# Half B's update gate in a gated recurrent kernel: sigmoid on ScalarE from PSUM, then a transpose on VectorE, in place of one joint transpose and two sigmoids

## The chip, the core and the metric

The kernel runs on one core of one Trainium2 chip. The metric is the device time of one execution in microseconds. Before the change it was 1668.68 us, the median of three runs (1668.61 to 1668.93).

## What is computed

The reference is a recurrent cell over 512 time steps for a batch of 8, with 512 inputs and 512 hidden units, whose states are added to the input:

```python
def step(h, x_t):
    fused = jax.nn.sigmoid(jnp.concatenate([x_t, h], axis=-1) @ w_W + w_b)
    hidden_state, output_state = jnp.split(fused, 2, axis=-1)
    memory_state = x_t @ wx_W + wx_b + hidden_state * (h @ wh_W + wh_b)
    h_new = output_state * h + (1.0 - output_state) * jnp.tanh(memory_state)
    return (h_new, h_new)
_, hs = jax.lax.scan(step, h0, xT)
x = x + jnp.swapaxes(hs, 0, 1)
```

Below, `r` is `hidden_state` before its sigmoid, `z` is `output_state` before its sigmoid, and the h part is `h @ wh_W + wh_b`. Everything is fp32. Each step needs the state of the step before, so 512 steps run one after the other.

## The kernel before the change

**Layouts.** A state is kept transposed, hidden units on the 128 partitions, because TensorE needs it so as its stationary operand. Each matmul has a 128x32 stationary tile, four of them side by side in the four column strips of the array, and its product comes out with batch rows on partitions (32 rows for each strip: 4 steps of a group by 8 batch elements). The gates must therefore be transposed back in blocks of 32x32 before they can be combined with the state; VectorE does that.

**Two halves.** The 512 hidden units are worked on in halves A and B of 256 units, so that one half's elementwise work can run beside matmuls that need the other half only. `hT[0]` is half A's state (hTA in the profile), `hT[1]` is half B's (hTB). The products go to three PSUM tiles for a group of four steps, and the x part of the next groups goes to two more (xp):

- A (256 columns): the h part of half B, the h part of half A from hTA, half A's z and r
- D (128 columns): half B's z (first 64 columns) and half B's r (last 64 columns)
- H (64 columns): the rest of half B's h part

**Order on TensorE.** Line 27 fixes it for every step: `ORDER = "A0 A1 A2 A3 D0 D1 D2 D3 H2 H3"`. The digit is the quarter of the state that is the stationary operand: 0 and 1 are half A, 2 and 3 half B. So A2 is the first matmul of a step that needs half B's new state. Behind H comes one piece of fill (line 397, `products`): x products for later steps, which wait for no state. In six of eight consecutive steps the fill piece is of one size, in the other two it is larger.

**Order on VectorE and ScalarE.** The scheduling is manual (line 187): every engine works off its instructions in the order in which the code issues them. Per step that is lines 485 to 512:

- `turn_r(0)`, `turn_h(0)`, `turn_z(0)`: three transposes of 64 columns out of tile A (tr, md1A, tz); ScalarE takes the sigmoid of each gate half into md0A and hd0A
- `memory(0, 0)`, `memory(0, 1)`: two scans (m<-md0A,md1A) that form r times h part plus x part; ScalarE takes tanh of each
- `turn_part`: a transpose of 64 columns out of A into md1B
- `turn_rz` (lines 455 to 464): one transpose of all 128 columns of D into the tile trz; ScalarE then takes the sigmoid of the r columns (8 of 32 columns, into md0B) and of the z columns (into hd0B), which are 16 elements per partition each
- `update(0, 0)`, `turn_h(1)`, `update(0, 1)`: the first and second scan of half A's new state (hTA<-hd0A,hTA), and between them the transpose of H (md1B<-H)
- `settle(1)` (line 446): a memset of one idle column that waits by semaphore until the transpose of H has written its result. It holds VectorE back until then, because what follows on the same engine reads that result
- `memory(1, 0)`, `memory(1, 1)`: the two scans m<-md0B,md1B, and ScalarE's two tanh behind them
- `update(1, 0)`, `update(1, 1)`: the two scans of half B's new state (hTB<-hd0B,hTB), each of which waits for its tanh

Behind these come pieces of the x work that differ from step to step, two more idle memsets (line 586), and GpSimd's output adds.

**Tiles that the change touches.** A `pair` (line 143) is a tile of 128 partitions by 2 quarters by a number of rows by 2 or 3 slots. hd0B has 8 rows and 3 slots, of which the scan of `update` reads all three, in the memory order row, slot. Its slot 2 holds the sigmoid of -z, that is 1 - sigmoid(z). A transpose into such a slot writes every third 4-byte word; one into half A's md1 (2 slots) writes every second. `IDLE` (line 23) is the width of the tile that the idle memsets write. `DVE_FILL` (line 22) says how many of the pairs are cleared by VectorE at the start.

In the profile one line stands for all uses of a helper: 195 is every matmul, 226 every activation, 403 every scan, 415 the transposes tr and tz, 430 the transposes of the h parts, 447 the settling memsets, 457 trz, 467 the transpose of the h part in A, 265 the transposes of x parts.

Of the kernel before, what the change touches and what calls it, by code (L numbers as in the profile page):

```python
# [7 lines left out]
F32 = mybir.dt.float32  # L8
BF16 = mybir.dt.bfloat16
AF = mybir.ActivationFunctionType  # L10
# [3 lines left out]
P = 128  # L14
NQ = 4
GS = 4
B = 8
HU = 64
# [1 line left out]


DVE_FILL = 23
IDLE = 4
LAST = 4
SYNC = mybir.DependencyInfo(mybir.DependencyClass.Sync, mybir.DependencyReason.DATA)

# [22 lines left out]
def tile_cond_rnn_residual(  # L49
# [39 lines left out]
    nc = tc.nc  # L89
# [7 lines left out]
    work = ctx.enter_context(tc.tile_pool(name="work", bufs=4))  # L97
# [45 lines left out]
    def pair(n, name, rows, slots):  # L143

        return const.tile([P, 2, rows, slots], F32, name=name).rearrange("p c n s -> p n c s")
# [3 lines left out]
    NH = 2 * GS  # L149
    hT = [[pair(n, f"hT{n}{i}", 32, 3) for i in range(NH)] for n in "AB"]  # L150

    md0 = [[pair(n, f"md0{n}{i}", 32, m) for i in range(2)] for n, m in (("A", 2), ("B", 3))]
    md1 = [[pair(n, f"md1{n}{i}", 32, m) for i in range(2)] for n, m in (("A", 2), ("B", 3))]
    hd0 = [[pair(n, f"hd0{n}{i}", B, 3) for i in range(2)] for n in "AB"]
    zeros = const.tile([P, 512], F32, name="zeros")
    nc.vector.memset(zeros, 0.0)
    none = const.tile([P, 128], BF16, name="none")
# [12 lines left out]
    for t_ in hd0[0] + hd0[1]:  # L170
        nc.gpsimd.memset(t_[:, :, :, 1], -1.0)
    idle = const.tile([P, IDLE], F32, name="idle")

# [8 lines left out]
    def state(hf, i, slot=2):  # L182

        s = i % GS
        return hT[hf][i % NH][:, B * s : B * s + B, :, slot]
# [39 lines left out]
    def act(key, out_, in_, func, **kw):  # L225
        inst = nc.scalar.activation(out_, in_, func, **kw).ins  # L226
        if key in written:
            tc.declare_no_dep(inst, written[key], reason="ordered through VectorE")
        written[key] = inst
        return inst  # L230
# [139 lines left out]
    for i in range(T):  # L370
        g, s = divmod(i, GS)
        c, t = divmod(i, TC)
        ps = banks[g % 2]
# [25 lines left out]
        rows = slice(B * s, B * s + B)  # L399

        def scan(c_, out_, d0, d1):

            return nc.vector.tensor_tensor_scan(  # L403
                *[t_[:, :, c_].rearrange("p n c s -> p (n c s)") for t_ in (out_, d0, d1)],
                0.0,
                ALU.mult,
                ALU.add,
            ).ins

        pa = ps["A"][:, HU:] if i else xps[0][:, :HALF]  # L410
        raw = {"h": (pa[:, :HU], ps["H"]), "z": (pa[:, HU : 2 * HU],), "r": (pa[:, 2 * HU :],)}

        def turned(n, hf):
            t_ = work.tile([P, 2, 32], F32, tag=f"t{n}{hf}", name=f"t{n}{hf}_{i}")
            inst = nc.vector.transpose(t_.rearrange("p c n -> p (c n)"), raw[n][hf]).ins  # L415
            return t_[:, :, rows], inst

        h_done = [None, None]

        def turn_r(hf):  # L420
            tr, _ = turned("r", hf)
            act(
                ("r", hf, g % 2, s),
                md0[hf][g % 2][:, rows, :, 1 + hf].rearrange("p n c -> p c n"),
                tr,
                AF.Sigmoid,
            )

        def turn_h(hf):
            inst = nc.vector.transpose(  # L430
                md1[hf][g % 2][:, :, :, hf].rearrange("p n c -> p c n"), raw["h"][hf]
            ).ins
            h_done[hf] = inst
            if hf == 0 and i + 1 - NH in pool_done:
                tc.add_manual_dep(inst, pool_done[i + 1 - NH].name, SYNC)

        def sigma_z(hf, tz):
            act(
                ("zc", hf, i % 2),
                hd0[hf][i % 2][:, :, :, 2].rearrange("p n c -> p c n"),  # L440
                tz,
                AF.Sigmoid,
                scale=-1.0,
            )

        def settle(hf):
            inst = nc.vector.memset(idle[:, IDLE - 2 + hf : IDLE - 1 + hf], 0.0).ins
            tc.add_manual_dep(inst, h_done[hf].name, SYNC)

        def turn_z(hf):  # L450
            tz, _ = turned("z", hf)
            settle(hf)
            sigma_z(hf, tz)

        def turn_rz():
            t_ = work.tile([P, 4, 32], F32, tag="trz", name=f"trz_{i}")
            nc.vector.transpose(t_.rearrange("p c n -> p (c n)"), ps["D"])  # L457
            act(
                ("r", 1, g % 2, s),
                md0[1][g % 2][:, rows, :, 2].rearrange("p n c -> p c n"),  # L460
                t_[:, 2:, rows],
                AF.Sigmoid,
            )
            sigma_z(1, t_[:, :2, rows])

        def turn_part():
            nc.vector.transpose(md1[1][g % 2][:, :, :, 0].rearrange("p n c -> p c n"), ps["A"][:, :HU])  # L467
# [6 lines left out]
        def memory(hf, q):  # L474

            c_ = slice(q, q + 1)
            scan(c_, ms[hf], md0[hf][g % 2][:, rows], md1[hf][g % 2][:, rows])
            act(("n", hf, q, i % NH), state(hf, i, 1)[:, :, c_], ms[hf][:, :, c_, 1 + hf], AF.Tanh)

        def update(hf, q):  # L480
            s1 = (i + 1) % GS
            new = hT[hf][(i + 1) % NH][:, B * s1 : B * s1 + B]
            return scan(slice(q, q + 1), new, hd0[hf][i % 2], hT[hf][i % NH][:, rows])

        turn_r(0)
        turn_h(0)
        turn_z(0)
        memory(0, 0)
        memory(0, 1)
        if i:  # L490
            turn_part()
        turn_rz()
        update(0, 0)
        turn_h(1)
        update(0, 1)
        settle(1)
        if i == 0:

            seed(2)
        memory(1, 0)  # L500
        if i == T - 1:
# [4 lines left out]
                ALU.add,  # L506
            )
        memory(1, 1)
        update(1, 0)
        update(1, 1)  # L510
        for hf in range(2):
# [70 lines left out]
        if i == 4:  # L582
            for to, c_ in ((Q01, slice(256, 448)), (Q23, slice(64, 256))):
                nc.vector.tensor_tensor(step_bias[to], bias[Q23, c_], bias[Q01, c_], ALU.subtract)
        for n in range(IDLE - 2):
            nc.vector.memset(idle[:, n : n + 1], 0.0)
        def add(hf, engine):
            return engine.tensor_tensor(  # L588
# [98 lines left out]
```

## Time and profile before

| what | value |
|---|---|
| time, median of 3 runs | 1668.68 us (1668.61 to 1668.93) |
| the profiled execution: its own time | 1665.8 us |
| the profiled execution: span from first to last instruction | 1664.0 us |
| granted TensorE clock | 1.000 of full speed |
| VectorE busy | 1391.8 us (84%), 10213 instructions |
| ScalarE busy | 1132.3 us (68%), 5884 instructions |
| GpSimd busy | 327.4 us (20%), 1290 instructions |

How to read the rows. A row of the timeline has a start in us, a length in us, the engine, the line, the operation, output<-input, shapes and a count; several instructions of one kind in a row are merged, and their length is that of all of them together. PE is TensorE's matmuls, PEld its weight loads, DVE VectorE, ACT ScalarE. What stands in square brackets is the idle time just before, and what ended it. A row of the groups by line has the total busy time, the mean length of one in ns, and the idle time before. A row of a tile's view has the shortest, median and longest length in ns. Matmuls overlap: four run side by side in the column strips and each is pipelined behind the one before it, so their lengths do not add up. VectorE's and ScalarE's instructions overlap too: the next may start some 0.04 to 0.1 us before the one in front of it has ended.

### The profile page before, as it was taken

How to read it: one execution, taken by the hardware profiler on the slowest of the kernel's cores; microseconds unless marked ns; L12 is line 12 of the kernel's file. 1: busy time of each engine (PE TensorE's matmuls, PEld its weight loads, DVE VectorE, ACT ScalarE, POOL GpSimd, SP SyncE). 2: the span in 40 equal slices, each digit the busy share in tenths (PEclk: the TensorE clock that was granted, in tenths of full speed). 3: DMA queues.
4: the chain of work that ended last, by engine and by line, in shares of the span. 5: the costliest groups of instructions: out<-in, count | busy, mean ns of one | idle time of the engine just before them, and what ended most of it. 6: DMA issues, size and time to landing. Idle time of an engine off the chain costs nothing.

```text
span 1664.0 us, 113147 instructions
## 1 busy us (share of the span) xinstructions
PE 1650.5 (99%) x47566; PEld 1272.1 (76%) x47566; DVE 1391.8 (84%) x10213; ACT 1132.3 (68%) x5884; POOL 327.4 (20%) x1290
## 2 busy tenths in 40 slices
PE   8999999999999999999999999999999999999998
PEld 5777777777777777777777777777777777777776
DVE  6888888888888888888888888888888888888886
ACT  4666666666666666666666666666666666666665
POOL 2211121211211212112112121121121211211211
PEclk9999999999999999999999999999999999999999
DMA  4000000000000000000000000000000000000000
GB/s 179 17 4 17 17 17 17 12 9 17 17 17 17 5 17 17 17 17 4 17 17 17 17 16 6 17 17 17 17 4 17 17 17 17 4 17 11 11 10 10
DMA packets 11464, 30.34 MB, mean 18 GB/s; under 512 B 1220, under 2 KB 1732, under 8 KB 10952
## 3 DMA queue, kind: packets, MB, share of 16 engines
q1 hardware_dynamic: 10800, 22.94, 4.0%
q8 instruction: 372, 6.09, 1.5%
q14 instruction: 140, 1.15, 0.2%
q10 hardware_dynamic: 152, 0.16, 0.0%
HBM read 14.70 MB, written 8.39 MB: 14 GB/s over the span
## 4 chain that ended last, share of the span: by engine, by line
PE 97%; DVE 2%; DMA 1%; issue 0%; ACT 0%; DVEq 0%
PE A L195 47%; PE D L195 26%; PE xp L195 17%; PE H L195 7%; DMA wd<-in_wd_dram 1%; DVE m L403 0%; DMA rows<-in_bias_dram 0%; DVE tr L415 0%; DVE trz L457 0%; DVE md1B L467 0%; DVE tw L283 0%; DVE md1A L430 0%; DVE tz L415 0%; DVE hTA L403 0%; DVE hTB L403 0%
## 5 line engine op out<-in xcount | busy, mean ns | idle before, releaser
L195 PE MATMUL A<-wa,hTA 128*32 128x256 f32 x8176 | 535.7, 379 | 3.7 <-DVE hTA L403 3.6
L195 PE MATMUL A<-wa,hTB 128*32 128x192 f32 x8176 | 437.8, 332 | 0.0
L195 PEld LDWEIGHTS A<-wa,hTA 128*32 128x32 f32 x8176 | 258.5, 122 | 175.9 <-DVE hTA L403 94.1
L588 POOL TENSOR_TENSOR ot<-xin,hTB 128x16 f32<-128x16 f32 x503 | 125.0, 248 | 1296.1 <-DVE hTB L403 1285.2
L195 PEld LDWEIGHTS A<-wa,hTB 128*32 128x32 f32 x8176 | 244.0, 124 | 154.8 <-DVE hTB L403 135.1
L195 PE MATMUL D<-wd,hTA 128*32 128x128 f32 x8192 | 317.9, 273 | 1.2 <-DMA wd<-in_wd_dram 1.2
L195 PE MATMUL D<-wd,hTB 128*32 128x128 f32 x8192 | 317.8, 273 | 0.0
L195 PE MATMUL xp<-tw,sx 128*32 128x192 f32 (+5 forms) x2480 | 276.3, 358 | 0.0
L195 PEld LDWEIGHTS D<-wd,hTA 128*32 128x32 f32 x8192 | 258.0, 122 | 21.8 <-DMA wd<-in_wd_dram 1.6
L226 ACT ACTIVATE md0A<-tr 128x16 f32<-128x16 f32 x512 | 112.8, 220 | 222.5 <-DVE tr L415 199.6
L195 PEld LDWEIGHTS D<-wd,hTB 128*32 128x32 f32 x8192 | 240.5, 122 | 0.0
L403 DVE TENSOR_TENSOR_SCAN hTB<-hd0B,hTB 128x24 f32<-128x24 f32 x1024 | 159.1, 197 | 94.3 <-ACT hTB L226 94.3
L415 DVE STREAM_TRANSPOSE tr<-A 128x64 f32<-128x64 f32 x511 | 127.5, 250 | 129.2 <-PE A L195 122.7
L226 ACT ACTIVATE hTB<-m 128x8 f32<-128x8 f32 x1024 | 163.5, 208 | 96.3 <-DVE m L403 96.2
L195 PE MATMUL xp<-wx,xin 128*32 128x384 f32 (+4 forms) x1552 | 218.9, 384 | 0.0
L195 PE MATMUL H<-wa,hTB 128*32 128x64 f32 x8192 | 208.5, 219 | 0.0
L195 PEld LDWEIGHTS H<-wa,hTB 128*32 128x32 f32 x8192 | 186.1, 122 | 0.0
L226 ACT ACTIVATE hTB<-hTB 128x16 f32<-128x16 f32 x512 | 121.6, 238 | 78.3 <-DVE hTB L403 62.8
L403 DVE TENSOR_TENSOR_SCAN hTA<-hd0A,hTA 128x24 f32<-128x24 f32 x1024 | 171.0, 167 | 0.0
L226 ACT ACTIVATE md0B<-trz 128x16 f32<-128x16 f32 x512 | 116.4, 227 | 73.5 <-DVE trz L457 12.0
L226 ACT ACTIVATE hTA<-m 128x8 f32<-128x8 f32 x1024 | 160.9, 206 | 2.4
L403 DVE TENSOR_TENSOR_SCAN m<-md0B,md1B 128x24 f32<-128x24 f32 x1024 | 154.4, 192 | 3.4
(102 smaller groups left out, 2630.3 us busy)
## 6 DMA issues: line engine op xcount, KB each, us to landing
xin<-in_x_dram SPq DMA_DIRECT2D x31, 256.0 KB, 3.3
out_dram<-ot SPq DMA_DIRECT2D x31, 256.0 KB, 2.0
wx<-in_wx_dram SPq DMA_DIRECT2D x4, 768.0 KB, 7.0
wa<-in_wa_dram SPq DMA_DIRECT2D x4, 512.0 KB, 9.8
wd<-in_wd_dram SPq DMA_DIRECT2D x1, 768.0 KB
wd<-in_wd_dram SPq DMA_DIRECT2D x1, 256.0 KB, 11.1
out_dram<-ot SPq DMA_DIRECT2D x1, 192.0 KB, 2.8
head<-in_xh_dram ACTq DMA_DIRECT2D x1, 144.0 KB, 5.0
```

What stands on the lines that cost most here:

```text
L195: nc.tensor.matmul(out_, lhsT, rhs, start=start, stop=False, skip_group_check=True)
L226: inst = nc.scalar.activation(out_, in_, func, **kw).ins
L403: return nc.vector.tensor_tensor_scan(*[t_[:, :, c_].rearrange("p n c s -> p (n c s)") for t_ in (out_, d0, d1)], 0.0, ALU.mult, ALU.add,).ins
L415: inst = nc.vector.transpose(t_.rearrange("p c n -> p (c n)"), raw[n][hf]).ins
L588: return engine.tensor_tensor(ot[:, t, 2 * hf : 2 * hf + 2, :].rearrange("p c n -> p n c"), x_of(c, slice(2 * hf, 2 * hf + 2), t, 1).rearr ...
```

## The change

Half A stays as it is; `turn_r`, `turn_z` and hd0A lose their parameter for the half. For half B, `turn_rz` is replaced by three things:

- VectorE transposes only the 64 r columns of D (tile tr, function `turn_r_b`), and ScalarE takes their sigmoid into md0B as before.
- ScalarE takes the sigmoid of -z from the 64 z columns of D in PSUM, untransposed, into a new SBUF tile sz (128x64, four buffers). This activation stands where the one into hd0B stood in ScalarE's order.
- VectorE transposes sz from SBUF into slot 2 of hd0B (`turn_sz`). In VectorE's order this stands behind `memory(1, 1)` and ahead of `update(1, 0)`. Behind the transpose comes a memset of one idle column that waits for the transpose's own semaphore, as `settle` does.

hd0B grows from 8 to 32 rows, since the transpose writes all 32; the scan reads the 8 rows of the step. The idle tile grows by a column.

```diff
-IDLE = 4
+IDLE = 5
...
-    hd0 = [[pair(n, f"hd0{n}{i}", B, 3) for i in range(2)] for n in "AB"]
+    hd0 = [[pair(n, f"hd0{n}{i}", m, 3) for i in range(2)] for n, m in (("A", B), ("B", 32))]
...
-        raw = {"h": (pa[:, :HU], ps["H"]), "z": (pa[:, HU : 2 * HU],), "r": (pa[:, 2 * HU :],)}
+        raw = {"h": (pa[:, :HU], ps["H"]), "z": (pa[:, HU : 2 * HU],), "r": (pa[:, 2 * HU :], ps["D"][:, HU:])}
...
-        def turn_rz():
-            t_ = work.tile([P, 4, 32], F32, tag="trz", name=f"trz_{i}")
-            nc.vector.transpose(t_.rearrange("p c n -> p (c n)"), ps["D"])
+        def turn_r_b():
+            t_, _ = turned("r", 1)
             act(
                 ("r", 1, g % 2, s),
                 md0[1][g % 2][:, rows, :, 2].rearrange("p n c -> p c n"),
-                t_[:, 2:, rows],
+                t_,
                 AF.Sigmoid,
             )
-            sigma_z(1, t_[:, :2, rows])
+            sz = work.tile([P, HU], F32, tag="sz", name=f"sz_{i}")
+            act(("sz", i % 4), sz, ps["D"][:, :HU], AF.Sigmoid, scale=-1.0)
+            return sz
+
+        def turn_sz(sz):
+            inst = nc.vector.transpose(
+                hd0[1][i % 2][:, :, :, 2].rearrange("p n c -> p c n"), sz
+            ).ins
+            mark = nc.vector.memset(idle[:, IDLE - 3 : IDLE - 2], 0.0).ins
+            tc.add_manual_dep(mark, inst.name, SYNC)
...
         def update(hf, q):
             s1 = (i + 1) % GS
             new = hT[hf][(i + 1) % NH][:, B * s1 : B * s1 + B]
-            return scan(slice(q, q + 1), new, hd0[hf][i % 2], hT[hf][i % NH][:, rows])
+            z_ = hd0[hf][i % 2][:, rows] if hf else hd0[hf][i % 2]
+            return scan(slice(q, q + 1), new, z_, hT[hf][i % NH][:, rows])
...
-        turn_rz()
+        sz = turn_r_b()
         update(0, 0)
         turn_h(1)
         update(0, 1)
...
         memory(1, 1)
+        turn_sz(sz)
         update(1, 0)
         update(1, 1)
...
-        for n in range(IDLE - 2):
+        for n in range(IDLE - 3):
             nc.vector.memset(idle[:, n : n + 1], 0.0)
```

`turned("r", 1)` transposes 64 columns into a work tile of 2x32 columns and returns the 8 columns of the step; `act` is one activation. On VectorE every step has two instructions more than before (a transpose and a memset); on ScalarE the count is the same.

More of the change, by code (lines that the diff above doesn't have):

```diff
@@ L418, in tile_cond_rnn_residual, with turn_r @@
         h_done = [None, None]
-        def turn_r(hf):
-            tr, _ = turned("r", hf)
-            act(
-                ("r", hf, g % 2, s),
-                md0[hf][g % 2][:, rows, :, 1 + hf].rearrange("p n c -> p c n"),
+        def turn_r():
+            tr, _ = turned("r", 0)
+            act(
+                ("r", 0, g % 2, s),
+                md0[0][g % 2][:, rows, :, 1].rearrange("p n c -> p c n"),
                 tr,
@@ L435, in turn_h, with settle, turn_z @@
                 tc.add_manual_dep(inst, pool_done[i + 1 - NH].name, SYNC)
-        def sigma_z(hf, tz):
-            act(
-                ("zc", hf, i % 2),
-                hd0[hf][i % 2][:, :, :, 2].rearrange("p n c -> p c n"),
+        def settle(hf):
+            inst = nc.vector.memset(idle[:, IDLE - 2 + hf : IDLE - 1 + hf], 0.0).ins
+            tc.add_manual_dep(inst, h_done[hf].name, SYNC)
+        def turn_z():
+            tz, _ = turned("z", 0)
+            settle(0)
+            act(
+                ("zc", i % 2),
+                hd0[0][i % 2][:, :, :, 2].rearrange("p n c -> p c n"),
                 tz,
@@ L444, in sigma_z @@
             )
[L446 to L453, printed above, removed]
-        def turn_rz():
-            t_ = work.tile([P, 4, 32], F32, tag="trz", name=f"trz_{i}")
-            nc.vector.transpose(t_.rearrange("p c n -> p (c n)"), ps["D"])
+        def turn_r_b():
+            t_, _ = turned("r", 1)
             act(
@@ L482, in update @@
             new = hT[hf][(i + 1) % NH][:, B * s1 : B * s1 + B]
-            return scan(slice(q, q + 1), new, hd0[hf][i % 2], hT[hf][i % NH][:, rows])
-        turn_r(0)
+            z_ = hd0[hf][i % 2][:, rows] if hf else hd0[hf][i % 2]
+            return scan(slice(q, q + 1), new, z_, hT[hf][i % NH][:, rows])
+        turn_r()
         turn_h(0)
-        turn_z(0)
+        turn_z()
         memory(0, 0)
```

## Prediction

> **What bounds the kernel now.** I read the page first. TensorE is busy throughout, and the chain that ended last is matmuls for 97% of the span:
>
> ```profile
> PE 1650.5 (99%) x47566; PEld 1272.1 (76%) x47566; DVE 1391.8 (84%) x10213; ACT 1132.3 (68%) x5884; POOL 327.4 (20%) x1290
> ...
> PE 97%; DVE 2%; DMA 1%; issue 0%; ACT 0%; DVEq 0%
> ```
>
> That suggests that work on VectorE can change nothing. But a busy TensorE may hold short stalls inside its matmuls, so I read the chain in order of time next, which gives the length of each block of matmuls:
>
> ```profile
> 808.38 0.54 PE xp L195 x8
> 808.92 1.54 PE A L195 x32
> ...
> 811.56 0.65 PE xp L195 x8
> 812.21 1.51 PE A L195 x32
> ...
> 814.81 0.65 PE xp L195 x8
> 815.46 1.51 PE A L195 x32
> ```
>
> The same 32 matmuls of block A take 1.54 us behind a fill piece of 0.54 us, and 1.51 us behind the larger pieces of 0.65 us, which come in two steps of eight. So some 0.03 us of A is a stall, in six of eight steps. The groups by line say where:
>
> ```profile
> L195 PE MATMUL A<-wa,hTB 128*32 128x192 f32 x8176 | 437.8, 332 | 0.0
> ...
> L195 PEld LDWEIGHTS A<-wa,hTB 128*32 128x32 f32 x8176 | 244.0, 124 | 154.8 <-DVE hTB L403 135.1
> ...
> L403 DVE TENSOR_TENSOR_SCAN hTB<-hd0B,hTB 128x24 f32<-128x24 f32 x1024 | 159.1, 197 | 94.3 <-ACT hTB L226 94.3
> ...
> L195 PE MATMUL xp<-tw,sx 128*32 128x192 f32 x992 | 63.4, 326 | 0.0
> ```
>
> A matmul of the same shape takes 326 ns where no state is awaited and 332 ns where half B's state is. Four run side by side, so the total stall is (332 - 326) ns x 8176 / 4 = **12.3 us**; 0.03 us x 6/8 x 512 steps = 11.5 us says the same. The first weight load that waits for hTB is A2's. So the first scan of half B's new state is late by about 0.03 us in 384 steps, and this is all that the change can win: earlier than that, TensorE itself is the bound.
>
> What makes it late is read from one step's timeline (first TensorE, then VectorE, ScalarE and the weight load):
>
> ```profile
> 806.41 0.87 PE L195 MATMUL A<-wa,hTB 128*32 128x192 f32 x16
> ...
> 807.54 0.62 PE L195 MATMUL D<-wd,hTB 128*32 128x128 f32 x16
> 807.97 0.41 PE L195 MATMUL H<-wa,hTB 128*32 128x64 f32 x16
> ```
>
> ```profile
> 807.35 0.25 DVE L415 STREAM_TRANSPOSE tr<-A 128x64 f32<-128x64 f32 x1 [0.19 <-PE A L195]
> ...
> 808.26 0.28 DVE L457 STREAM_TRANSPOSE trz<-D 128x128 f32<-128x128 f32 x1
> 808.46 0.17 DVE L403 TENSOR_TENSOR_SCAN hTA<-hd0A,hTA 128x24 f32<-128x24 f32 x1
> 808.55 0.25 DVE L430 STREAM_TRANSPOSE md1B<-H 128x64 f32<-128x64 f32 x1
> 808.69 0.17 DVE L403 TENSOR_TENSOR_SCAN hTA<-hd0A,hTA 128x24 f32<-128x24 f32 x1
> 808.85 0.20 DVE L403 TENSOR_TENSOR_SCAN m<-md0B,md1B 128x24 f32<-128x24 f32 x1
> 808.87 0.06 DVE L447 MEMSET idle<- 128x1 f32 x1
> 808.97 0.18 DVE L403 TENSOR_TENSOR_SCAN m<-md0B,md1B 128x24 f32<-128x24 f32 x1
> 809.33 0.31 DVE L403 TENSOR_TENSOR_SCAN hTB<-hd0B,hTB 128x24 f32<-128x24 f32 x2 [0.18 <-ACT hTB L226]
> ```
>
> ```profile
> 808.57 0.23 ACT L226 ACTIVATE md0B<-trz 128x16 f32<-128x16 f32 x1
> 808.70 0.21 ACT L226 ACTIVATE hd0B<-trz 128x16 f32<-128x16 f32 x1
> 809.08 0.32 ACT L226 ACTIVATE hTB<-m 128x8 f32<-128x8 f32 x2 [0.17 <-DVE m L403]
> ```
>
> ```profile
> 809.59 0.19 PEld L195 LDWEIGHTS A<-wa,hTB 128*32 128x32 f32 x8 [0.28 <-DVE hTB L403]
> ```
>
> The path: D's matmuls end at 807.54 + 0.62 = 808.16, trz ends at 808.54, the transpose of H ends at 808.80, the first scan m of half B starts 0.05 later, its tanh follows, and hTB starts at 809.33, **0.48 us after m**. The weight load follows within 0.3 us. Between the second m and hTB VectorE has a gap of 0.18 us, in which it waits for tanh: the change puts its new work there.
>
> **The change, part by part.**
>
> ```profile
> L415 DVE STREAM_TRANSPOSE tr<-A x511: 238/250/251, 22.2 to 1658.8; 128x64 f32<-128x64 f32 x171
> ...
> L457 DVE STREAM_TRANSPOSE trz<-D x512: 272/307/317, 19.2 to 1659.7; 128x128 f32<-128x128 f32 x171
> ...
> L430 DVE STREAM_TRANSPOSE md1B<-H x512: 228/254/314, 19.7 to 1660.0; 128x64 f32<-128x64 f32 x171
> L467 DVE STREAM_TRANSPOSE md1B<-A x511: 246/253/320, 22.9 to 1659.6; 128x64 f32<-128x64 f32 x171
> L265 DVE STREAM_TRANSPOSE md1B<-xs x254: 195/204/215, 24.4 to 1645.2; 128x32 f32<-128x32 f32 x127
> ...
> L430 DVE STREAM_TRANSPOSE md1A<-A x511: 202/209/215, 22.4 to 1659.0; 128x64 f32<-128x64 f32 x171
> ```
>
> *r alone.* A transpose of 64 columns that waits for TensorE takes 250 ns (tr), the one of 128 took 307 ns: 0.057 us less. In the step above, tr ends 0.32 us behind A's last matmul (806.41 + 0.87 = 807.28; 807.60), trz 0.38 us behind D's: 0.06 us again. I take **-0.06**. What follows (hTA, the transpose of H, hTA, m) stands back to back behind it and moves with it, if nothing else is late. Next to be late would be H: its matmuls end at 808.38, and with the 0.07 us from A's end (807.28) to tr (807.35), the transpose of H could start at 808.45; moved, it would start at 808.49. The sigmoid of r waits for the transpose only and moves with it too.
>
> *sz on ScalarE.* It takes hd0B's place in the order. The trace has no sigmoid of 64 columns from PSUM; ScalarE's copies give a slope of (378 - 271) ns / 128 columns:
>
> ```profile
> L260 ACT COPY A<-xs 128x256 f32<-128x256 f32 x127 | 48.0, 378 | 0.7
> L260 ACT COPY D<-xs 128x128 f32<-128x128 f32 x127 | 34.4, 271 | 1.5
> ```
>
> So 0.21 + 48 columns x 0.84 ns = 0.25 us; bounds 0.21 (no slope) and 0.27 (the copy of 128 columns). From 808.70 - 0.06 it runs to 808.89. The transpose that needs it comes at 809.00 (next term) and tanh at 809.02. Cost nothing; what hides it is the scans m, with about 0.1 us to spare.
>
> *The transpose of sz.* It follows the second m. A transpose starts 0.09 us after the scan ahead of it (808.46, 808.55). Its length: the trace has no transpose of 64 columns from SBUF into every third word. From below, the 204 ns of md1B<-xs, which has half the columns; from above, the longest of its like from PSUM, 314 and 320 ns. Half of (307 - 250) ns, for 32 columns more, on top of 204 ns gives 0.23; the medians of the like rows from PSUM are 0.253 and 0.254. I take 0.25, the nearer in size and in the pattern written.
>
> *The memset that waits for it.* After the transpose of H the settling memset does the same, and from that transpose's end to the scan behind it there are 0.05 us (808.80 to 808.85). I take 0.05, bounds 0.03 to 0.06 (a memset's own length). Behind this memset stand both scans of hTB, all of VectorE's later work of the step, and TensorE's A2.
>
> So from the first m to hTB: 0.12 (808.85 to 808.97) + 0.09 + 0.25 + 0.05 = 0.51 us, where tanh let hTB start after 0.48. **+0.03**. Together with -0.06, hTB comes **0.03 us earlier**: with the bounds of the transpose (0.20 to 0.32) between 0.06 us earlier (there tanh is the limit again) and 0.04 us later.
>
> *Rest.* hd0B's two clears at the start, 98 ns each, grow from 48 elements to 192; even at four times that they add 0.6 us, once, beside the loads of the weights: nothing. TensorE's D now waits for sz of the step before as well, done over 1 us earlier: nothing.
>
> ```profile
> L167 DVE MEMSET hd0B<- x2: 98/98/98, 2.8 to 2.9; 128x48 f32 x2
> ```
>
> *The sum.* 0.03 us x 384 stalled steps = 11.5 us, nearly all of the 12.3 us that are there. The profiled execution's 1665.8 us would become 1654.3. It was 2.9 us below the median of the runs; from that median, 1668.7 - 11.5 = **1657.2 us**.
>
> **Where the Trainium skill speaks against it.** The rows md1A<-A (every second word written) and md1B<-A (every third) differ by 44 ns. The Trainium skill's Vector Engine (DVE) Microarchitecture Reference, § Measured stream behaviour on trn2, says that a port keeps its full rate only where elements come in runs of two or more adjacent words, and measures 1.71 to 2.51 ns per column in place of 1.05 for scattered writes. By that an estimate for 64 columns is 42 to 93 ns above a dense write. The trace agrees for every third word and not for every second (tr writes densely, md1A does not, and md1A is no longer). My 0.25 has it in it as far as the like rows have. The Trainium skill's VectorE: DVE Perf Modes, § Rules for kernel authors, advises to minimize the count of operations, as each pays its own flush; here two more come in per step. By that, the gap of 0.18 us is not free; rival B is this.
>
> **The rivals.**
>
> *A, half of it.* The transpose takes 0.265 us, or the memset's wait 0.065: hTB comes 0.015 us earlier, 5.8 us in all: 1662.9. For it: md1B<-H's median of 254 has a tail to 314. Against: the source is SBUF, and the row from SBUF is at 204.
>
> *B, the gap doesn't hold the transpose: slower.* Two operations more per step, of which the transpose writes scattered words, at the 314 to 320 ns of the slowest like rows: 0.12 + 0.09 + 0.32 + 0.05 = 0.58 against 0.48, less 0.06, is 0.04 us later, x 384 = 15 us: 1684. It decides from a transpose of 0.28 us on. For it: the long rows exist. Against: they are a minority, as the medians show.
>
> *C, the gain at r doesn't arrive: slower.* If half B's first m cannot come earlier (H's matmuls or the sigmoid of r hold it), only the +0.03 stays: 11.5 us slower, 1680. H would have to release VectorE later than 0.11 us after its end to bite, and 0.17 us to take all; A's end takes 0.07.
>
> *D, both cancel:* 1668.7.
>
> **How the numbers follow.** About 0.2%, 3.3 us, can be told from no change. Forecast (1653.5 to 1660): 0.55. A (1660 to 1665.3): 0.17. D, within 3.3 us: 0.08. B 0.14 and C 0.06, slower by more. So faster 0.72, same 0.08, slower 0.20. The likeliest case's own range is 1653.5 to 1660; it reaches 3 us below the 1656.4 that the 12.3 us would give, since some of the stall may lie in other blocks. The range for all, 1653.5 to 1675, leaves out the worse parts of B and C (0.16) and little below.
>
> **What would show it.** Right: block A at 1.51 us in all steps, A<-wa,hTB at a mean near 326 ns, the transpose of sz near 0.25 us, the first m 0.06 us sooner behind D's end, hTB's wait for ACT gone and in its place the memset. Wrong: A longer than 1.55 us (B or C), the transpose above 0.28 us (B), an unchanged time from D's end to m (C), or a stall in another block that takes the place of A2's.

## The result and the profile after

| | before | after |
|---|---|---|
| time, median | 1668.64 us (4 runs, 1668.58 to 1668.93) | **1657.73 us** (4 runs, 1657.29 to 1659.18) |
| after/before | | 0.9936, 95% interval 0.9919 to 0.9953 |
| the profiled execution: its own time | 1665.8 us | 1659.18 us |
| its span | 1664.0 us | 1657.4 us |

The kernel is 10.9 us faster; 1657.2 was predicted. Two further sets of five runs each gave 1657.60 and 1657.79 us (below).

The page of the changed kernel, busy time by engine:

```profile
PE 1646.6 (99%) x47566; PEld 1295.7 (78%) x47566; DVE 1439.3 (87%) x11237; ACT 1137.5 (69%) x5884; POOL 328.5 (20%) x1290
```

VectorE does 1024 instructions more and is busy 47 us longer, in a kernel that is 11 us shorter. The page's shares told nothing about this change, before it or after it.

The groups by line, the changed kernel (total us, mean ns of one | idle before it and its releaser):

```profile
L195 PE MATMUL A<-wa,hTB 128*32 128x192 f32 x8176 | 430.8, 328 | 0.0
...
L403 DVE TENSOR_TENSOR_SCAN hTB<-hd0B,hTB 128x24 f32<-128x24 f32 x1024 | 154.6, 193 | 21.8
L465 DVE STREAM_TRANSPOSE hd0B<-sz 128x64 f32<-128x64 f32 x512 | 126.7, 247 | 0.0
...
L226 ACT ACTIVATE sz<-D 128x64 f32<-128x64 f32 x512 | 106.8, 209 | 1.5
```

The matmuls that need half B's state take 328 ns (332 before; 326 with nothing to wait for). The 94.3 us in which the scan of hTB waited for tanh are gone: the transpose and its memset fill that gap. But 328 is not 326: some stall is left.

Where it is left shows in the chain in order of time; these are the A blocks of eight consecutive steps of the changed kernel (start us, length us):

```profile
800.09 1.51 PE A L195 x32
...
803.25 1.51 PE A L195 x32
...
806.40 1.53 PE A L195 x32
...
809.67 1.51 PE A L195 x32
...
812.92 1.51 PE A L195 x32
...
816.07 1.56 PE A L195 x32
...
819.27 1.51 PE A L195 x32
...
822.42 1.53 PE A L195 x32
```

Five of eight blocks stand at 1.51 us, the length without a stall; before, two did. Three still wait, one of them as long as ever (1.56). Over the whole trace 322 of the 507 blocks that the chain gives stand at 1.51.

A step in which the change works, the changed kernel's timeline ahead of the block at 803.25:

```profile
801.86 0.62 PE L195 MATMUL D<-wd,hTB 128*32 128x128 f32 x16
...
802.55 0.24 DVE L415 STREAM_TRANSPOSE tr<-D 128x64 f32<-128x64 f32 x1
...
802.81 0.25 DVE L430 STREAM_TRANSPOSE md1B<-H 128x64 f32<-128x64 f32 x1
802.83 0.22 ACT L226 ACTIVATE md0B<-tr 128x16 f32<-128x16 f32 x1
802.95 0.21 ACT L226 ACTIVATE sz<-D 128x64 f32<-128x64 f32 x1
...
803.10 0.20 DVE L403 TENSOR_TENSOR_SCAN m<-md0B,md1B 128x24 f32<-128x24 f32 x1
...
803.32 0.25 DVE L465 STREAM_TRANSPOSE hd0B<-sz 128x64 f32<-128x64 f32 x1
...
803.60 0.20 DVE L403 TENSOR_TENSOR_SCAN hTB<-hd0B,hTB 128x24 f32<-128x24 f32 x1
```

D's matmuls end at 801.86 + 0.62 = 802.48. The transpose of r ends 0.31 us later (0.38 for trz), the first m starts 0.62 us after D's end (0.69), and hTB starts 0.50 us after m (0.48). hTB is 1.12 us behind D's end where it was 1.17. sz is there at 803.16, ahead of its transpose at 803.32, which ends 0.03 us ahead of the scan that waits for its write.

A step in which it does not work, ahead of the block at 816.07, same kernel and view:

```profile
814.69 0.62 PE L195 MATMUL D<-wd,hTB 128*32 128x128 f32 x16
...
815.63 0.29 DVE L430 STREAM_TRANSPOSE md1B<-H 128x64 f32<-128x64 f32 x1
815.66 0.24 ACT L226 ACTIVATE md0B<-tr 128x16 f32<-128x16 f32 x1
...
815.93 0.22 ACT L226 ACTIVATE sz<-D 128x64 f32<-128x64 f32 x1
815.97 0.20 DVE L403 TENSOR_TENSOR_SCAN m<-md0B,md1B 128x24 f32<-128x24 f32 x1
...
816.19 0.27 DVE L465 STREAM_TRANSPOSE hd0B<-sz 128x64 f32<-128x64 f32 x1
...
816.50 0.20 DVE L403 TENSOR_TENSOR_SCAN hTB<-hd0B,hTB 128x24 f32<-128x24 f32 x1
...
816.75 0.87 PE L195 MATMUL A<-wa,hTB 128*32 128x192 f32 x16
...
817.69 0.25 DVE L415 STREAM_TRANSPOSE tr<-A 128x64 f32<-128x64 f32 x1
```

Here the transpose of H takes 0.29 instead of 0.25 us, so m starts 0.66 us behind D's end (815.31). sz starts 0.27 us behind the sigmoid of r instead of 0.12, and ends at 816.15, just ahead of its transpose, which takes 0.27. hTB comes 0.53 us after m and 1.19 us after D's end: as late as before the change.

The other two places that still wait differ. Ahead of the block at 822.42 the transpose of H takes 0.29 us as well (at 821.99 in the same view). Ahead of the one at 806.40 it takes 0.25, but VectorE comes to r's transpose 0.03 us later than elsewhere and starts H's transpose that much later. Long transposes of H were in the profile before the change too, but in the two steps of eight with the larger fill piece, where TensorE does not wait for hTB; one of them, ahead of the block at 812.21 that the prediction shows at 1.51 us:

```profile
811.74 0.31 DVE L430 STREAM_TRANSPOSE md1B<-H 128x64 f32<-128x64 f32 x1
```

In the changed kernel they stand in two of the six steps with the smaller fill piece. What makes them long is not shown.

### The profile page after: what moved, and what is told of

Same layout as the page of the kernel before. It is cut to its first block, busy times and chain, and to the rows that moved or that the text cites. A ratio compares the mean times of both kernels' runs of the same rounds, so it can differ in the third digit from the quotient of the medians.

```text
span 1657.4 us, 114239 instructions
## 1 busy us (share of the span) xinstructions
PE 1646.6 (99%) x47566; PEld 1295.7 (78%) x47566; DVE 1439.3 (87%) x11237; ACT 1137.5 (69%) x5884; POOL 328.5 (20%) x1290
## 4 chain that ended last, share of the span: by engine, by line
PE 97%; DVE 2%; issue 0%; ACT 0%; DVEq 0%
PE A L195 47%; PE D L195 26%; PE xp L195 18%; PE H L195 7%; DVE m L403 0%; DVE tr L415 0%; DVE md1B L472 0%; DVE tw L283 0%; DVE md1A L430 0%; DVE hTA L403 0%; DVE tz L415 0%; DVE hTA L167 0%; DVE hTB L167 0%; DVE hTB L403 0%; DVE md1B L430 0%
## 5 line engine op out<-in xcount | busy, mean ns | idle before, releaser
L195 PE MATMUL A<-wa,hTB 128*32 128x192 f32 x8176 | 430.8, 328 | 0.0
L195 PEld LDWEIGHTS A<-wa,hTA 128*32 128x32 f32 x8176 | 270.0, 122 | 166.0 <-DVE hTA L403 81.6
L195 PEld LDWEIGHTS A<-wa,hTB 128*32 128x32 f32 x8176 | 258.1, 123 | 133.4 <-DVE hTB L403 103.5
L403 DVE TENSOR_TENSOR_SCAN hTA<-hd0A,hTA 128x24 f32<-128x24 f32 x1024 | 175.9, 172 | 0.0
L403 DVE TENSOR_TENSOR_SCAN hTB<-hd0B,hTB 128x24 f32<-128x24 f32 x1024 | 154.6, 193 | 21.8
L403 DVE TENSOR_TENSOR_SCAN m<-md0A,md1A 128x16 f32<-128x16 f32 x1024 | 142.3, 181 | 8.6
```

The lines of the kernel that those rows point to most:

```text
L195: nc.tensor.matmul(out_, lhsT, rhs, start=start, stop=False, skip_group_check=True)
L403: return nc.vector.tensor_tensor_scan(*[t_[:, :, c_].rearrange("p n c s -> p (n c s)") for t_ in (out_, d0, d1)], 0.0, ALU.mult, ALU.add,).ins
```

## The experiments

The theory after the result: all of the time is the stall ahead of A2; r alone brings hTB 0.06 us forward, and the new work behind m gives a part of that back, since the scan is held until the transpose has written, and not since VectorE is busy with the transpose. Rivals: the gain comes from something other than r; the new work costs nothing, and what is left has another cause; or the split of z from r pays by itself, wherever z is turned.

**The changed kernel again**, twice, beside the others:

> The changed kernel once more, on the chip of the next three, so that they can be compared with it closely. Expected 1657.7 us within 1.5 us, and stalls ahead of A2 left in one to three steps of eight.

1657.60 us, ratio 0.9934 (0.9921 to 0.9946).

> The changed kernel again, on the chip of the next two: 1657.6 us within 1 us.

1657.79 us, ratio 0.9935 (0.9923 to 0.9948). The result stands.

**The new work on VectorE left out.** Half B's z then stays at zero, so the states are not the reference's.

```diff
         memory(1, 1)
-        turn_sz(sz)
         update(1, 0)
```

> Leaves out the transpose of sz and the memset behind it, so half B's z stays at zero and the states are not the reference's; everything else as in the changed kernel. My theory (they stand on the path by some 0.03 us per step, since they end after tanh): hTB starts 0.48 us after the first m again, the stall ahead of A2 goes, 3 to 5 us less than the changed kernel, about 1653.5 us. Rival (the gap hides them wholly, and what stall is left has another cause): the same as the changed kernel within 1 us.

1653.94 us, ratio 0.9911 (0.9897 to 0.9924). So the transpose and its memset cost 3.7 us together, and without them nothing of the stall is left, in the groups by line of this kernel:

```profile
L195 PE MATMUL A<-wa,hTB 128*32 128x192 f32 x8176 | 427.0, 326 | 0.0
```

The rival that the rest has another cause falls: H's longer transposes are in this kernel as well (259 ns on average, as in the changed one), and without the new work they are covered.

**The transpose without the wait for its write.** It goes to a spare tile, as long and in the same pattern, and nothing waits for it.

```diff
-            inst = nc.vector.transpose(
-                hd0[1][i % 2][:, :, :, 2].rearrange("p n c -> p c n"), sz
-            ).ins
-            mark = nc.vector.memset(idle[:, IDLE - 3 : IDLE - 2], 0.0).ins
-            tc.add_manual_dep(mark, inst.name, SYNC)
+            nc.vector.transpose(spare[i % 2][:, :, :, 2].rearrange("p n c -> p c n"), sz)
```

> The transpose of sz stays, but writes into a spare tile that nobody reads, and the memset that waits for it is left out; half B's z stays at zero, so the states are not the reference's. It parts the transpose's own time on VectorE from the wait for the end of its write. My theory (VectorE could go on 0.14 us after the transpose's start, and 0.12 + 0.10 + 0.14 = 0.36 us from the first m is less than tanh's 0.48; the price of the changed kernel is the wait for the write): 1654 us, as without the transpose. Rival (the transpose itself pushes hTB): 1657 to 1658 us, as the changed kernel.

1654.0 us, ratio 0.9913 (0.9899 to 0.9926), the time without the transpose. The groups by line of this kernel have it in full:

```profile
L466 DVE STREAM_TRANSPOSE spare<-sz 128x64 f32<-128x64 f32 x512 | 127.3, 249 | 0.0
```

249 ns of VectorE per step are free here. The timeline of this kernel shows hTB 0.49 us behind m, as before the change:

```profile
803.37 0.20 DVE L404 TENSOR_TENSOR_SCAN m<-md0B,md1B 128x24 f32<-128x24 f32 x1
...
803.86 0.31 DVE L404 TENSOR_TENSOR_SCAN hTB<-hd0B,hTB 128x24 f32<-128x24 f32 x2
```

So the 3.7 us come from holding the scan until the transpose has written. In the changed kernel the transpose starts 0.22 us behind m and ends after 0.25 us more, at 0.47, ahead of the 0.49 at which tanh lets hTB start; only the 0.04 us from its end to the scan stand out, by 0.02. This run takes away the wait and the memset that carries it together; the next one keeps both.

**The wait shortened.** The transpose of sz in two pieces of 32 columns; each scan waits, by a memset of its own, for its own piece.

```diff
         def turn_sz(sz):
-            inst = nc.vector.transpose(
-                hd0[1][i % 2][:, :, :, 2].rearrange("p n c -> p c n"), sz
-            ).ins
+            return [
+                nc.vector.transpose(hd0[1][i % 2][:, :, q, 2], sz[:, 32 * q : 32 * q + 32]).ins
+                for q in range(2)
+            ]
...
-        turn_sz(sz)
-        update(1, 0)
-        update(1, 1)
+        halves = turn_sz(sz)
+        for q in range(2):
+            mark_sz(halves[q])
+            update(1, q)
```

> The transpose of sz in two pieces of 32 columns, one for each quarter, back to back behind the second m; each of the two scans of hTB waits by a memset for its own piece only. Two VectorE instructions more per step. My theory (what delays the first hTB is the wait for the end of the write; the first piece ends 0.04 us sooner, and the second scan has room): hTB's first scan 0.48 to 0.49 us after the first m, the second 0.12 us behind it as before, the stall ahead of A2 mostly gone, 1653.8 to 1655.5 us. Rival (two operations more in the gap cost as much as they save, or delay the second scan): 1657 us or more.

**1653.65 us, ratio 0.9913 (0.9900 to 0.9927):** 4.1 us below the changed kernel, with two instructions more per step. One step of its timeline:

```profile
803.14 0.20 DVE L403 TENSOR_TENSOR_SCAN m<-md0B,md1B 128x24 f32<-128x24 f32 x1
...
803.36 0.29 DVE L466 STREAM_TRANSPOSE hd0B<-sz 128x32 f32<-128x32 f32 x2
...
803.63 0.21 DVE L403 TENSOR_TENSOR_SCAN hTB<-hd0B,hTB 128x24 f32<-128x24 f32 x1
803.76 0.20 DVE L403 TENSOR_TENSOR_SCAN hTB<-hd0B,hTB 128x24 f32<-128x24 f32 x1
```

Both pieces together take 0.29 us, more than the one of 0.25, but the first scan waits for the first piece only: 0.49 us after m, where tanh lets it start anyway. The memsets, two of them here, cost nothing that shows.

**The transpose between the two scans m**, so that its write lands earlier; the memset that waits stays behind the second.

```diff
         memory(1, 0)
+        sz_done = turn_sz(sz)
...
         memory(1, 1)
-        turn_sz(sz)
+        mark_sz(sz_done)
         update(1, 0)
```

> The transpose of sz stands between the two scans m of half B, and the memset that waits for it behind the second. My theory: the first hTB depends on the first m alone, so it starts 0.48 us after it as in the kernel before, and the second m and the second hTB, which has room until A3, carry the delay of 0.1 to 0.15 us: 2 to 4 us less than the changed kernel, about 1654.5 us. Rival one (the gap hid the transpose anyway): the same within 1 us. Rival two (the second hTB has no room): slower than the changed kernel by more than 5 us, with A3 stalled.

1672.82 us, ratio 1.0024 (1.0014 to 1.0033): slower than both kernels. I had expected 1654.5; that theory fell. The timeline of this kernel, in the same place of the eight steps as the one ahead of the block at 816.07 above:

```profile
822.21 0.20 DVE L403 TENSOR_TENSOR_SCAN m<-md0B,md1B 128x24 f32<-128x24 f32 x1
...
822.41 0.27 DVE L465 STREAM_TRANSPOSE hd0B<-sz 128x64 f32<-128x64 f32 x1
...
822.58 0.17 DVE L403 TENSOR_TENSOR_SCAN m<-md0B,md1B 128x24 f32<-128x24 f32 x1
822.72 0.20 DVE L403 TENSOR_TENSOR_SCAN hTB<-hd0B,hTB 128x24 f32<-128x24 f32 x1
...
822.99 0.87 PE L195 MATMUL A<-wa,hTB 128*32 128x192 f32 x16
823.03 0.21 DVE L403 TENSOR_TENSOR_SCAN hTB<-hd0B,hTB 128x24 f32<-128x24 f32 x1
823.27 0.56 DVE L538 TENSOR_TENSOR u<-xp,u 64x384 f32<-64x384 f32 x1
...
824.13 0.25 DVE L415 STREAM_TRANSPOSE tr<-A 128x64 f32<-128x64 f32 x1
```

The first hTB did come nearly as expected, 0.51 us after m here and 0.48 to 0.49 in the other seven places. But the second m is late, with it the second tanh and the second hTB (0.31 us behind the first), and so all that VectorE does in the rest of the step. Where a long x piece follows (u, 0.56 us), VectorE reaches the next step's tr at 824.13, 0.27 us behind the end of A's matmuls (822.99 + 0.87 = 823.86); in the changed kernel it did so 0.07 us behind them (816.75 + 0.87 = 817.62; 817.69). The next step's VectorE work starts late by that, half A's as well as half B's, and the A block behind it carries both waits, in the chain of this kernel:

```profile
825.50 1.67 PE A L195 x32
```

That half A's state is late too shows in the mean of A<-wa,hTA, 382 ns against 379 in the changed kernel. Two places of eight lose by this, and make 0.25 of the 0.31 us that the A blocks of eight steps last beyond 1.51 us. Rival two was near in the time but not in the place: A3, which it named, follows A2 as in the other kernels, and A2 or the matmuls ahead of it wait.

**The same, with sz freed of a wait.** In the step that is left over sz starts late on ScalarE. One candidate was a wait of sz on ScalarE's own copy of the x part into D; it is declared unnecessary here, on top of the edit before.

```diff
+            put[n, g % 2] = nc.scalar.copy(
...
-            act(("sz", i % 4), sz, ps["D"][:, :HU], AF.Sigmoid, scale=-1.0)
+            inst = act(("sz", i % 4), sz, ps["D"][:, :HU], AF.Sigmoid, scale=-1.0)
+            tc.declare_no_dep(inst, put["D", g % 2], reason="ordered through TensorE")
```

> As the kernel with the transpose between the scans, and ScalarE's sigmoid into sz no longer waits for ScalarE's own copy into D of the group (TensorE's matmuls are ordered behind that copy, and the sigmoid behind them). In the changed kernel's profile this second wait stands as an instruction of its own in one step of eight, and the sigmoid starts 0.26 us after the one before it rather than 0.12. My theory: that step's transpose comes 0.03 us sooner, 64 x 0.02 = 1.3 us less than without, about 1653.2 us. Rival (the own wait is free once satisfied, the late start has another cause): the sigmoid starts as late as before in that step, and the time is the same within 0.5 us.

1672.69 us, ratio 1.0023 (1.0014 to 1.0032): no difference. The 1653.2 expected here rested on the theory that had fallen with the run before, and the time alone tells little, as this kernel stalls elsewhere. Its timeline does: in that place sz still starts 0.26 us behind the sigmoid of r (821.98 and 822.24). That wait isn't what delays sz.

**r's part undone.** All 128 columns of D are transposed as before; sz and its transpose stay.

```diff
-            t_, _ = turned("r", 1)
+            t_ = work.tile([P, 4, 32], F32, tag="trz", name=f"trz_{i}")
+            nc.vector.transpose(t_.rearrange("p c n -> p (c n)"), ps["D"])
...
-                t_,
+                t_[:, 2:, rows],
```

> Undoes the short transpose: VectorE transposes all 128 columns of D again and the sigmoid of r reads that tile; the sigmoid from PSUM into sz, its transpose and the memset stay as changed. My theory (the gain is the 0.06 us that r's shorter transpose takes off the path, and the new work costs 0.03 us): hTB 0.03 us later than in the kernel before, 1676 to 1682 us. Rival (the gain comes from taking z's sigmoid off the tile trz, the length of the transpose is nothing): as the changed kernel, 1657 to 1659 us.

1677.35 us, ratio 1.0046 (1.0031 to 1.0061). The time expected came. So r alone is worth 19.6 us in this kernel (against the 1657.73 of the changed one), and the rest of the change by itself costs 8.2 us (against 1669.16 of the kernel before beside it). The groups by line of this kernel have trz back at 301 ns:

```profile
L454 DVE STREAM_TRANSPOSE trz<-D 128x128 f32<-128x128 f32 x512 | 154.3, 301 | 1.5 <-PE D L195 1.5
```

**The split by itself.** In the kernel before, trz becomes two transposes of 64 columns, r and then z, both from PSUM and both ahead of the scans of hTA.

```diff
-            nc.vector.transpose(t_.rearrange("p c n -> p (c n)"), ps["D"])
+            nc.vector.transpose(t_.rearrange("p c n -> p (c n)"), ps["D"][:, HU:])
+            tz = work.tile([P, 2, 32], F32, tag="tz1", name=f"tz1_{i}")
+            nc.vector.transpose(tz.rearrange("p c n -> p (c n)"), ps["D"][:, :HU])
```

> The kernel before, with its transpose of D split in two of 64 columns, r first and z right behind it, and the two sigmoids as before: r alone is transposed, but z is not moved off the path. My theory (what stands on the path is VectorE's time from D's end to the first m): two transposes cost 0.13 us more from start to start and 0.06 less for the first, 0.07 us later in all, 1690 to 1702 us. Rival (the gain is that r's sigmoid starts sooner): 1657 to 1664 us.

1699.01 us, ratio 1.0178 (1.0161 to 1.0195). The gain does not come from the split by itself: z's transpose must also leave the place ahead of the scans. On average over the trace the first m starts 0.77 us behind D's end here, against 0.70 and 0.71 in the two profiles of the kernel before, and hTB follows it by 0.49 as before. Part of the loss lies in half A: z's transpose stands ahead of the scans of hTA as well, and A<-wa,hTA takes 386 ns in place of 379.

**The sigmoid behind the transpose.** z is transposed raw from PSUM in the gap; the sigmoid follows on ScalarE, behind tanh.

```diff
-            act(("sz", i % 4), sz, ps["D"][:, :HU], AF.Sigmoid, scale=-1.0)
...
+            nc.vector.transpose(tz.rearrange("p c n -> p (c n)"), ps["D"][:, :HU])
+            act(
+                ("zb", i % 2),
+                hd0[1][i % 2][:, rows, :, 2].rearrange("p n c -> p c n"),
+                tz[:, :, rows],
```

> The other order for z: VectorE transposes z raw from PSUM at the place where sz is transposed, and ScalarE takes the sigmoid of it behind its two tanh; r as changed. My theory (the sigmoid must be done ahead of the transpose, because behind it stands only the update): hTB 0.23 to 0.25 us later than in the changed kernel, all steps stalled, 1750 to 1770 us. Rival (the place of the transpose is what counts): 1657 to 1675 us.

1761.57 us, ratio 1.0553 (1.0537 to 1.0568). A step's timeline in this kernel:

```profile
858.01 0.23 ACT L226 ACTIVATE hd0B<-tz 128x16 f32<-128x16 f32 x1
...
858.27 0.31 DVE L403 TENSOR_TENSOR_SCAN hTB<-hd0B,hTB 128x24 f32<-128x24 f32 x2 [0.29 <-ACT hd0B L226]
```

Here hTB waits for the sigmoid. That the sigmoid goes first, untransposed, is what lets z's transpose stand last.

**The transpose twice**, first into a spare tile.

```diff
         def turn_sz(sz):
+            nc.vector.transpose(spare[i % 2][:, :, :, 2].rearrange("p n c -> p c n"), sz)
             inst = nc.vector.transpose(
```

> The changed kernel with the transpose of sz done twice, first into a spare tile of the same pattern, then into hd0B. My theory (the gap is used up, so each further nanosecond there is paid): 0.13 to 0.15 us later in each step, less a little slack in the two steps of eight with larger fill, 1706 to 1720 us. Rival (the gap has room): below 1665 us.

1703.01 us, ratio 1.0202 (1.0187 to 1.0217), a little less than expected. The gap has no room for a second one. The timeline of this kernel:

```profile
826.46 0.20 DVE L404 TENSOR_TENSOR_SCAN m<-md0B,md1B 128x24 f32<-128x24 f32 x1
...
826.82 0.23 DVE L467 STREAM_TRANSPOSE hd0B<-sz 128x64 f32<-128x64 f32 x1
...
827.09 0.20 DVE L404 TENSOR_TENSOR_SCAN hTB<-hd0B,hTB 128x24 f32<-128x24 f32 x1
```

hTB is 0.63 us behind m, 0.13 more than with one transpose.

**The kernel before, profiled again.** Its first profile was 2.9 us below its own median, and the two profiles differed by 6.6 us where the medians differ by 10.9.

> The kernel before the change, profiled once more. Its profiled execution took 1665.8 us, 2.9 us less than the median of its runs (1668.6 to 1669.2), while those of the other kernels lie within 1.5 us of theirs; so the traces show 8 us of gain (steps' sum, and the mean of A<-wa,hTB from 332 to 328 ns: 8.2 us) and the medians 10.9. Theory: this was one execution in which the stall was smaller than usual; an ordinary one, of 1668.5 us and more, has the 2.9 us in the same place: A<-wa,hTB at a mean of 333 to 334 ns (2.9 us x 4 / 8176 = 1.4 ns more), and the first full step starts at 20 us as before. Rival: the difference lies outside the steps, at the start or the end: A<-wa,hTB stays at 332 ns and the first full step starts, or the last output lands, some 2 to 3 us later. If this execution takes 1665.8 us again, nothing is told.

This execution took 1669.89 us; the 19 timed runs of this kernel in the first set of experiments lie between 1668.41 and 1670.41. The tile's view of it (shortest, median and longest in ns, first and last start in us):

```profile
L195 PE MATMUL A<-wa,hTA x8176: 378/379/421, 21.4 to 1661.8; 128*32 128x256 f32 x200
```

In the first profile these matmuls, with which a step begins, ran from 20.1 to 1657.7. Of the 4.1 us between the two, 1.3 came ahead of the first full step and 2.8 in the steps. In the changed kernel's profile they run from 21.4 to 1651.0, so against this one the steps gained 10.8 us, which is what the medians say. The three blocks that waited longest among eight, in the chain of this execution:

```profile
805.30 1.56 PE A L195 x32
808.50 1.55 PE A L195 x32
811.69 1.59 PE A L195 x32
```

My number for it, a mean of 333 to 334 ns, failed: the mean of A<-wa,hTB stayed at 332. The block's length shows the stall in full; the mean length of a matmul does not. When A2 is late, its first four matmuls are longer, up to some 366 ns in place of 326; what goes beyond that shows as a later start of A2 behind the last matmul of A1, 0.23 us in place of 0.20 in the place that waits longest here, and is no part of any matmul's length. That place is also where most of the added 2.8 us lie, and there the transpose of H takes 0.29 us in this execution and 0.25 in the first.

**All together.** For each kernel, what eight consecutive A blocks last beyond 1.51 us, from its chain in order of time, times 64 for 512 steps; the sum of the same over the A blocks of the whole trace; and what its profiled execution took above 1653.9 us (the middle one of the times of the three kernels without a stall: 1653.65, 1653.94, 1654.0):

| kernel | excess in 8 steps, us | x 64 | whole trace, us | own time - 1653.9 |
|---|---|---|---|---|
| before, first profile | 0.19 | 12.2 | 12.7 | 11.9 |
| before, second profile | 0.27 | 17.3 | 15.4 | 16.0 |
| changed | 0.09 | 5.8 | 4.8 | 5.3 |
| without the new work | 0.01 | 0.6 | 0.8 | 0.1 |
| transpose without the wait | 0.00 | 0.0 | 0.7 | -0.1 |
| two pieces | 0.01 | 0.6 | 0.7 | -0.3 |
| between the scans m | 0.31 | 19.8 | 19.7 | 18.8 |
| r's part undone | 0.35 | 22.4 | 22.8 | 22.0 |
| split by itself | 0.73 | 46.7 | 44.7 | 45.1 |
| transpose twice | 0.76 | 48.6 | 48.8 | 49.0 |

The sum over the whole trace has 505 to 507 of the 511 blocks of each kernel; it leaves out a dozen, nearly all at the end, that last 1.74 us or more in every kernel. The excess of one block accounts for these times to within 1.6 us from eight steps, and 1.0 us from the whole trace. That the three kernels without a stall come out near zero is built in; that the others follow is not. In the rows of the split and of the transpose between the scans, the block's excess has waits for half A's state in it too. The kernel with the sigmoid last is not in the table, as its chain leaves the A blocks; from a step's first A matmul to the end of its last it takes 1.91 us on average, 1.70 where nothing waits, and 0.21 x 512 = 108 us stands against 107.7.

The kernel without that stall takes some 1653.9 us. As the A blocks then stand at 1.51 us, nothing that VectorE and ScalarE do in front of A2 is seen to wait any more.

## Why the prediction was right, point by point

- **The bound** was right for this change: the stall ahead of A2, and nothing else. Its size was not: 12.3 us were read from an execution that stalled less than most. From the median there were 1668.6 - 1653.9 = 14.7 us to win. To subtract a gain that was read in one execution from the median of others was the weak step. Of the 4.1 us between the two profiles of the kernel before, 2.8 lie in the steps, where the stall is, and 1.3 ahead of the first. The formula from the mean lengths, 332 against 326 ns, was no measure either: it gives the same 12.3 us for the second profile, and that it came near in the first was luck.
- **r alone, -0.06 us,** was right: the transpose's end moved from 0.38 to 0.31 us behind D's end (0.384 to 0.317 on average over the traces), and undoing it alone costs 19.6 us.
- **sz hidden** was right: 209 ns on average (0.25 taken). In one place of eight it starts 0.15 us later than elsewhere and ends with only 0.04 us to spare, but its transpose starts there as soon behind the second m as elsewhere.
- **The transpose, 0.25 us,** measured 247 ns, 265 in that one place. **The memset's wait, 0.05 us,** measured 0.04 from the transpose's end to the scan. So from m to hTB it is 0.50 to 0.51 us in seven places of eight (0.51 predicted) and 0.53 in the one ahead of the block at 816.07.
- **Net 0.03 us in each of 384 steps** was right as a mean only. On average over the six steps with the smaller fill piece, hTB moved from 1.175 and 1.183 us behind D's end (the two profiles before) to 1.146. But where the change works, hTB is 0.05 us earlier; in two places of eight it gains nothing or next to nothing, because the transpose of H grew from 0.25 to 0.29 us there, which the prediction's "moves with it" left out. The time gained 10.9 us where 11.5 was forecast because two errors went against each other, which was luck: 2.4 us more were there than I counted, and 3.8 us were left lying where I had 0.8 (12.3 - 11.5).
- **The signs named** held in part: block A is at 1.51 us in five places of eight and not in all, and in one place it is at 1.56, above the 1.55 that was to speak for B or C.
- **Rival A** (half of it, as the transpose takes 0.265 us) is seen in one place of eight, together with the longer transpose of H; the time of 1662.9 did not come. **B** has its mechanism shown, not its case: with a gap overfull by 0.13 us the kernel takes 1703. **C** did not happen in most places: H's transpose starts 0.10 us behind H's end, just short of the 0.11 from which it would bite. In two places it starts at 0.13, as VectorE comes later, and one of them still waits. **D**, no change, lies outside the measured interval.
- **What a page of the Trainium skill would have made of it.** The Trainium skill's VectorE: DVE Perf Modes, § Rules for kernel authors, advises to minimize the count of operations. The kernel with the most VectorE operations per step of all here, the one in two pieces, is the fastest of those that compute the whole reference. In the gap, transpose and memset were free as work; what had a price was the wait for a write in front of the instruction that TensorE waits for, a second transpose that overfilled the gap, and a transpose that pushed the second m back.

What stays open: why H's transpose takes 0.29 to 0.31 us in some places of eight and 0.25 in others, and why sz starts late in one place. The long transposes stand in the steps with the larger fill piece in the kernel before (in its second profile in one step of eight besides) and in the split, and in two of the other steps in the changed kernel and its variants, save the one that writes to the spare tile without a wait, which has hardly any. No run here singles out the cause; the kernel in two pieces covers both.

## What to carry to other kernels

Where an engine reads 99% busy, take the length of one repeated block from the chain, step by step, and compare it with the same block where it waits for nothing: the excess times the number of steps is what can be won. Work that is put in a gap on an engine that works in order costs nothing for being there; it costs what it makes the next consumer wait beyond what that waits for anyway, and what it pushes back behind it. So, where its write comes a little late, cut it to let the first consumer wait for the first piece, and look past the next consumer to the end of the engine's step. Read the size of a small stall from more than one execution ahead of a forecast.

## What had not been expected of the hardware

- Two executions of the same kernel differed by 4.1 us (1665.8 and 1669.89). Of these, 1.3 came ahead of the first full step and 2.8 in the steps. In the second the transposes of H took 272 ns on average, in the first 266; that this makes the longer stall was not tried.
- A transpose of 128x64 from SBUF into every third word took 247 ns, with one like it right ahead 229 (the second of the two). Two of 128x32 took 0.29 us together, against 0.25 for one of 128x64.
- The sigmoid of 128x64 from PSUM took 209 ns on ScalarE, no more than the one of 128x16 from SBUF that it replaces (211 in the kernel before).
